# Two expert layers on one core: the first weights in eight chunks on two queues

## The chip, the core and the metric

The kernel runs on one core of one Trainium2 chip. A core has TensorE (PE, matrix products), VectorE (DVE), ScalarE (ACT), GpSimd (POOL) and SyncE (SP), which only issues transfers here. Transfers (DMAs) are issued from SyncE and ScalarE and run on 16 DMA engines that the two share. The metric is the device time of one execution in microseconds (us); less is better.

## The reference

There are 128 samples x of 128 rows and 1024 columns, and for each sample a role among three (the values 1 and 2 occur). Two layers follow each other; each picks its weights by the sample's role:

```python
h = einsum('bsh,bhk->bsk', x, W_down[role]) + b_down[role]   # 1024 -> 512
h = gelu(h)
u = einsum('bsk,bkh->bsh', h, W_up[role]) + b_up[role]       # 512 -> 1024
y = x + u
x = layernorm(y) * gamma[role] + beta[role]
```

All numbers are float32. The second layer has weights of its own and the same form.

## The kernel before, in words

**Tiling.** The samples are sorted by role on the chip and taken in pairs of one role, 63 full pairs and one pair of left-over samples. The run has four phases: down and up of the first layer, down and up of the second. A phase goes over all pairs. The product of a pair is computed by a scheme of seven half-size products in place of eight, from sums of parts of x (`Sd`, written by `winograd_sums`, L418 to L421, mostly on GpSimd) and of parts of the weights (`T1` to `T4`, written for the first phase by `first_sum`, L171, on VectorE). Weights of three "places", one for each role in order of frequency, live in the tile `wall`.

**The first pair is special.** Its role is the most frequent one (`role_0`), and its two samples are the first two with it (`first_two`), both known early. It is computed plainly (`plain`, L576 to L594): for each of the two samples a bias product (L584, one row), then eight products of 128 by 128 with 128 by 512 (L587), each with the next block j of 128 rows of W_down; then the activation on ScalarE (L591). A float32 product is two passes on TensorE, so the profile counts 16 for a sample. The weights for this come in two transfers of 1 MB, `load_rows(0, ...)` on ScalarE's queue and `load_rows(1, ...)` on SyncE's (L148): partition p holds rows 8p to 8p + 7 of W_down, of which each transfer takes four. x comes in four transfers of 128 KB for each sample (`quartered`, L404, in rows of 1 KB), and VectorE turns it (L547, `turn`), for the first pair in halves of four blocks.

**Sorting.** Before that, VectorE works out the order of the samples in some 40 short steps (L274 to L361). Three results come through TensorE by `gathered` (a product, L338, and a copy to a row, L340): `perm` (which sample sits in which slot), `role_of` (which role has which place) and `place` (which place a slot has; read only from the 22nd pair on). Between these, `zeros` (L262) issues products of zeros into banks whose results nobody reads.

**Order.** The order of the work is written out by hand: `at(time, step)` (L835) puts a step on a list, the list is emptied in order of time, and each instruction is bound to follow the one before it on its engine (L987). The units of time are steps, seven to a pair, and say nothing of microseconds. The code that sorts runs before the list. The steps at the head of the first phase:

```python
at(-31, lambda: load_rows(0, 0, nc.scalar))
at(-30.5, load_bias_row)
at(-29, lambda: load_rows(1, 0, nc.sync))
at(-26, lambda: load_bias([0], nc.scalar))
at(0.3, lambda: subtract(slice(0, 1)))
for t, name in zip((-8.7, -2.5, 4.6, 4.7), ("T1", "T2", "T3", "T4")):
```

(L961 to L966.) x of the first pair is issued at steps -30 and -28, of the second and third pair from -19 on. Transfers carry one of eight semaphores, by turns, and a transfer waits before it is issued until the one that last had its semaphore has landed; so about eight are under way at a time.

Of the kernel before, what the change touches and what calls it, by code (L numbers as in the profile page):

```python
# [13 lines left out]
ALU = mybir.AluOpType  # L14
ENG = mybir.EngineType
# [4 lines left out]
P = 128  # L20
SQ = 32
NQ = P // SQ
# [4 lines left out]
def kernel(  # L27
# [29 lines left out]
    nc = tc.nc  # L57
    B, S, H = x.shape
    R, _, K = layers[0][0].shape
# [25 lines left out]
    def flat(tag, bufs, name, size=2048):  # L85
        return work.tile([P, size], F32, tag=tag, name=name, bufs=bufs)
# [51 lines left out]
    rows_of = [  # L138
        wall[:, 2 * k : 2 * k + 2]
        .rearrange("p k n -> p (k n)")  # L140
        .rearrange("p (r j h c) -> p r j h c", r=R, h=2, c=K // 2)
        for k in range(2)
    ]

    def load_rows(k, place, queue):
        role = reg(role_of, place, [queue.engine], R - 1) if place else reg(role_0, 0, [queue.engine], R - 1)
        src = layers[0][0][ds(role, 1)].rearrange("o (p m) c -> p (o m) c", p=P)
        queue.dma_start(rows_of[k][:, place].rearrange("p j h c -> p j (h c)"), src[:, ts(k, NQ)])  # L148

    first_weights = {  # L150
        "B11": Half(rows_of[0], 0),
# [8 lines left out]
    def first_sum(name, place):  # L160
        b11, b12, b21, b22 = (rows_of[k][:, :, :, h] for k in range(2) for h in range(2))
        t1, t2, t4 = (
            first_weights[n].v.rearrange("p r (j c) -> p r j c", c=K // 2) for n in ("T1", "T2", "T4")
        )
        o, a, b = {
            "T1": (t1, b12, b11),
            "T2": (t2, b22, t1),
            "T3": (b12, b22, b12),
            "T4": (t4, b21, t2),
        }[name]  # L170
        nc.vector.tensor_tensor(o[:, place], a[:, place], b[:, place], ALU.subtract)  # L171

    class Sums:
# [85 lines left out]
    def zeros(tags):  # L259
        for t in tags:  # L260
            ps = psum.tile([P, 512], F32, tag=t, name=f"{t}_zero", bufs=3)
            nc.tensor.matmul(ps, zero[:, 0:P], zero[:, 0:512], start=True, stop=True)  # L262
# [3 lines left out]
    def bank_a(name):  # L266
        return psum.tile([P, 512], F32, tag="a", name=name, bufs=2)
# [4 lines left out]
    iota_r, ones_r = iota_row[:, 0:R], ones[:, 0:R]  # L272
# [18 lines left out]
    ps = bank_a("row_ps")  # L291
    nc.tensor.matmul(ps[:, 0 : B + 2 * R], ones[0:1, 0:P], row[0:1], start=True, stop=True)

    zeros("bbbbbbbb")
    role_row, key = ps[:, 0:B], f32(R)
    counts = f32(R + 1)

# [3 lines left out]
    role_0 = const.tile([1, 1], I32, name="role_0")  # L301
# [8 lines left out]
    role_col, rank, own_key = f32(1), f32(1), f32(1)  # L310
# [18 lines left out]
    onehot = f32(B)  # L329
# [4 lines left out]
    def gathered(name, values, where):  # L334

        ps = bank_a(name + "_ps")
        n = where.shape[1]
        nc.tensor.matmul(ps[0:SQ, 0:n], values, where, start=True, stop=True)  # L338
        t = const.tile([1, n], I32, name=name)
        nc.vector.tensor_copy(t, ps[0:1, 0:n])  # L340
        return t

    perm = gathered("perm", wide, onehot)
    zeros("bbb")

    place_r, key_r, at_place = f32(1)[0:R], f32(1)[0:R], f32(R)[0:R]
    nc.vector.tensor_scalar(at_place, iota_r[0:R], iota_col[0:R], None, ALU.is_equal)
# [7 lines left out]
    role_of = gathered("role_of", wide[0:R], at_place)  # L355
    zeros("bbb")

    own_place, wide_place = f32(1), f32(SQ)
    counted(own_place, key, own_key, ALU.is_gt, ones_r)
    nc.vector.tensor_copy(wide_place, own_place.to_broadcast((P, SQ)))  # L360
    place = gathered("place", wide_place, onehot)  # L361
    zeros("bbbb")

    def reg(t, s, engines, top):
        return nc.values_load(
            t[0:1, s : s + 1],
            engines=engines,
            min_val=0,
            max_val=top,
            skip_runtime_bounds_check_because="computed on the chip, always in this range",  # L370
        )

    def set_places(item, engines):

        n = item.n
        if n < NFIRST:
            item.places = [0, 0]
        elif n < NPAIR:
            item.places = [reg(place, 2 * n, engines, R - 1)] * 2
        else:  # L380
            item.places = [reg(place, 2 * n + s, engines, R - 1) for s in range(2)]

    def samples(n, engine):
        return [reg(perm, 2 * n + s, [engine], B - 1) for s in range(2)]
# [11 lines left out]
    first_rows = const.tile([P, 1, K], F32, name="first_rows")  # L396
    bias_row = first_rows[0:1, 0]

    def quartered(t, srcs):

        for s, src in enumerate(srcs):
            n = src.shape[-1] // NQ
            for q in range(NQ):
                nc.sync.dma_start(  # L404
                    t[s][ts(q, SQ)], src[:, ts(q, n)].rearrange("(a t) c -> t a c", t=SQ)
                )

    def x_of(layer, n, engine):
        if layer:
            return [mid[n][s] for s in range(2)]  # L410
        return [x[ds(i, 1)].rearrange("o s h -> (o s) h") for i in samples(n, engine)]
# [26 lines left out]
    def bank(t, tag):  # L438
        return psum.tile([P, 512], F32, tag=t, name=f"{t}{tag}", bufs=BANKS[t])
# [77 lines left out]
    class Down:  # L517
# [7 lines left out]
        def load(self):  # L525
            if self.among_weights:


                block = self.ph.weights[ORDER[self.m]].v
                self.xq = [block[:, 1 + s] for s in range(2)]  # L530
            else:
                self.xq = [flat("q", 4, f"xq{self.tag}_{s}", H) for s in range(2)]
            self.xq = [t.rearrange("p (a c) -> p a c", a=NQ) for t in self.xq]
            if self.early:
                quartered(self.xq[0:1], [self.early_x(0, ENG.SP)])
                return
            self.srcs = x_of(self.layer, self.n, ENG.SP)
            quartered(self.xq[0:1], self.srcs[0:1])

        def load_rest(self):  # L540
            quartered(self.xq[1:2], [self.early_x(1, ENG.SP)] if self.early else self.srcs[1:2])
# [34 lines left out]
        def plain(self):  # L576


            self.ps = [None, None]

            def half(s, k):
                if k == 0:
                    self.ps[s] = bank("a", f"{self.tag}_{s}")
                    nc.tensor.matmul(self.ps[s], ones[0:1, 0:P], bias_row, start=True, stop=False)  # L584
                for j in range(NQ):
                    rows = rows_of[k][:, 0, j].rearrange("p h c -> p (h c)")
                    nc.tensor.matmul(  # L587
                        self.ps[s], self.a[:, s, NQ * k + j], rows, start=False, stop=k == 1 and j == NQ - 1
                    )
                if k == 1:  # L590
                    nc.scalar.activation(self.h[s], self.ps[s], AF.Gelu)  # L591

            steps = [(4 * s + 2 * k, lambda s=s, k=k: half(s, k)) for s in range(2) for k in range(2)]
            return steps + [(0.1 + k / 10, lambda k=k: self.turn(1, ts(k, NQ))) for k in range(2)]  # L594

        def products(self):
            return [(-0.5, self.first)] + (self.plain() if self.early else item_products(self, K // 2))
# [237 lines left out]
    def at(time, step):  # L835
        heapq.heappush(events, (time, next(count_), step))
# [117 lines left out]
    ph = phases[0]  # L954
    ph.bias, load_bias, subtract = bias_table(ph.vectors[0], 2)

    def load_bias_row():
        r = reg(role_0, 0, [ENG.Activation], R - 1)
        nc.scalar.dma_start(bias_row, ph.vectors[0][ds(r, 1), :])

    at(-31, lambda: load_rows(0, 0, nc.scalar))  # L961
    at(-30.5, load_bias_row)
    at(-29, lambda: load_rows(1, 0, nc.sync))
    at(-26, lambda: load_bias([0], nc.scalar))
    at(0.3, lambda: subtract(slice(0, 1)))
    for t, name in zip((-8.7, -2.5, 4.6, 4.7), ("T1", "T2", "T3", "T4")):  # L966
        at(t, lambda name=name: first_sum(name, 0))
    at(14.7, lambda: load_bias(range(1, R)))
    at(20.7, lambda: subtract(slice(1, R)))
# [48 lines left out]
```

## Time and profile before

| What | Value |
|---|---|
| median of 3 runs | 3129.63 us (3129.15 to 3130.18) |
| the profiled execution | 3130.06 us |
| its span in the profile | 3128.3 us |
| TensorE busy | 3112.7 us (99%) |
| VectorE busy | 1975.8 us (63%) |
| GpSimd busy | 1777.3 us (57%) |
| first pass of the first pair's product | at 15.02 us |
| first pass of the second pair's product | at 31.81 us |
| TensorE clock from 16 to 19 us | 0.50 of full |

In lines of the timeline the first number is the start, the second the time to the end of the group, both in us; then the engine (`PEld` is the load of TensorE's stationary operand, `SPq` and `ACTq` are issues of transfers), the line of the kernel, the operation, what it writes and reads, the shape, and in brackets how long the engine was idle before and what it then waited for. Lines of waits give the engine and line that waited, whom for, the total in us, the times and the longest.

### The profile page before, as it was taken

To read this page: it belongs to the slowest core of one execution; us is meant where nothing else is said; L and a number is where in the kernel's file an instruction comes from. 1 tells how busy PE (TensorE), PEld (TensorE's weight loads), DVE (VectorE), ACT (ScalarE), POOL (GpSimd) and SP (SyncE) were. 2 spreads that over 40 slices of the span, in tenths; PEclk is the share of its full clock that TensorE was granted. 3 is DMA by queue.
4 is the path that set the end of the run, shared out by engine and by line. 5 is a ranking of instruction groups with operands and counts; after the bars stand their busy time and mean duration, and the time that the engine had idled before them with its cause. 6 is when DMAs were issued, how large, how long until landed. Compare 5 with 4: busy or idle time off the path is not lost.

```text
span 3128.3 us, 42229 instructions
## 1 busy us (share of the span) xinstructions
PE 3112.7 (99%) x10796; PEld 2047.8 (65%) x10796; DVE 1975.8 (63%) x2807; ACT 1203.5 (38%) x2816; POOL 1777.3 (57%) x1391
## 2 busy tenths in 40 slices
PE   9999999999999999999999999999999999999999
PEld 6888888888544444444478888888884444444443
DVE  6554544544678777777864444444447877777777
ACT  1222222222454555454432222222224545454544
POOL 3545344444577767777654343444436777677775
PEclk9999999999999999999999999999999999999999
DMA  8778788876786565656687555555567765656564
GB/s 218 196 216 209 212 206 210 213 209 196 272 288 240 211 227 208 225 212 226 225 224 179 146 130 131 130 127 138 126 183 275 280 239 206 227 207 226 211 227 176
DMA packets 429735, 642.21 MB, mean 205 GB/s; under 512 B 35778, under 2 KB 305603, under 8 KB 428356
## 3 DMA queue, kind: packets, MB, share of 16 engines
q1 hardware_dynamic: 428930, 637.15, 66.2%
q8 instruction: 102, 1.67, 0.2%
q10 hardware_dynamic: 578, 2.36, 0.2%
q14 instruction: 125, 1.02, 0.1%
HBM read 405.02 MB, written 234.36 MB: 204 GB/s over the span
## 4 chain that ended last, share of the span: by engine, by line
PE 49%; POOL 1%; issue 0%; DMA 0%; SPq 0%; DVE 0%; ACT 0%; DVEq 0%; POOLq 0%; ACTq 0%
PE bu L427 14%; PE bd L427 14%; PE eu L427 7%; PE ed L427 7%; PE au L427 3%; PE ad L427 3%; POOL ou L809 0%; SPq L404 0%; DMA hd<-hd 0%; POOL Sd L420 0%; POOL Sd L418 0%; DMA wall<-mid 0%; POOL varu L794 0%; POOL xTd L419 0%; DVE ou L712 0%
## 5 line engine op out<-in xcount | busy, mean ns | idle before, releaser
L427 PE MATMUL bu<-wall,hTu 128*128 (+1 forms) x2048 | 921.3, 592 | 0.0
L547 DVE STREAM_TRANSPOSE xTd<-xqd 128x1024 f32<-128x1024 f32 (+1 forms) x252 | 504.9, 2071 | 350.7 <-PE bd L427 283.8
L427 PEld LDWEIGHTS bu<-wall,hTu 128*128 128x128 f32 x2048 | 389.1, 190 | 487.2 <-issue 456.6
L418 POOL TENSOR_TENSOR Sd<-xTd 128x512 f32<-128x512 f32 x124 | 159.7, 1288 | 790.4 <-DVE xTd L547 782.7
L794 POOL TENSOR_TENSOR varu<-varu,mhalf 128x1 f32<-128x1 f32 x254 | 329.6, 1298 | 393.8 <-ACT varu L793 393.8
L427 PE MATMUL bd<-wall,xTd 128*128 (+1 forms) x2064 | 487.1, 379 | 1.8 <-ACT bd L445 1.8
L427 PE MATMUL eu<-wall,hTu 128*128 (+1 forms) x1040 | 488.0, 592 | 0.0
L427 PE MATMUL bd<-wall,Sd 128*128 (+1 forms) x2000 | 472.8, 379 | 2.2 <-ACT hd L606 1.6
L427 PEld LDWEIGHTS bd<-wall,xTd 128*128 128x128 f32 x2064 | 392.0, 190 | 57.5 <-ACT bd L445 2.6
L427 PEld LDWEIGHTS bd<-wall,Sd 128*128 128x128 f32 x2000 | 379.7, 190 | 56.5 <-issue 2.6
L801 DVE SCALAR_TENSOR_TENSOR ou<-xu,meanu,tables 128x1024 f32<-128x1024 f32 x253 | 325.3, 1286 | 138.3 <-ACT ou L792 120.0
L611 ACT ACTIVATE hd<-hd 128x256 f32<-128x256 f32 x379 | 157.6, 416 | 534.5 <-DVE hd L610 534.4
L427 PEld LDWEIGHTS eu<-wall,hTu 128*128 128x128 f32 x1040 | 197.6, 190 | 247.4 <-issue 218.8
L788 ACT ACTIVATE partu<-statu 128x2 f32<-128x2 f32 x254 | 51.6, 203 | 728.7 <-DVE xu L690 728.7
L809 POOL TENSOR_TENSOR ou<-ou,tables 128x1024 f32<-128x1024 f32 x126 | 296.9, 2356 | 0.0
L792 ACT ACTIVATE ou<-xu,meanu 128x1024 f32<-128x1024 f32 x254 | 291.7, 1148 | 8.4
L681 DVE TENSOR_TENSOR xu<-bu,xu 128x512 f32<-128x512 f32 x256 | 176.1, 688 | 119.1 <-PE bu L427 119.1
L427 PE MATMUL ed<-wall,xTd 128*128 (+1 forms) x1064 | 251.0, 379 | 0.0
L418 POOL TENSOR_TENSOR hTu<-hTu 128x256 f32<-128x256 f32 x126 | 198.1, 1572 | 70.8 <-DVE hTu L656 49.0
L427 PE MATMUL au<-wall,hTu 128*128 (+1 forms) x504 | 236.8, 592 | 0.0
L427 PE MATMUL ed<-wall,Sd 128*128 (+1 forms) x1000 | 236.3, 379 | 0.1
L427 PE MATMUL ad<-wall,xTd 128*128 (+1 forms) x1000 | 236.2, 379 | 0.0
(135 smaller groups left out, 3383.1 us busy)
## 6 DMA issues: line engine op xcount, KB each, us to landing
xqd<-in_x_dram SPq DMA_DIRECT2D x512, 128.0 KB, 3.3
hd<-hd SPq DMA_DIRECT2D x256, 256.0 KB, 2.4
xu<-in_x_dram SPq DMA_DIRECT2D x128, 512.0 KB, 3.8
mid<-ou SPq DMA_DIRECT2D x128, 512.0 KB, 4.2
xu<-mid SPq DMA_DIRECT2D x128, 512.0 KB, 3.8
out_dram<-ou SPq DMA_DIRECT2D x125, 512.0 KB, 3.8
hqu<-hd SPq DMA_DIRECT2D x244, 256.0 KB, 5.0
xqd<-mid SPq DMA_DIRECT2D x488, 128.0 KB, 3.8
```

What stands on the lines that cost most here:

```text
L418: engine.tensor_tensor(dst[:, 1], a11, a21, ALU.subtract)
L427: nc.tensor.matmul(ps[:, 0:cols], a[:, j], w.rhs(r, j, cols), start=start and j == 0, stop=j == n - 1, skip_group_check=True,)
L547: nc.vector.transpose(self.a[:, s, chunks].rearrange("p j (t a) -> p j a t", t=SQ), self.xq[s].rearrange("p a (i j) -> p j a i", i=SQ)[:, ...
L611: nc.scalar.activation(y, y, AF.Gelu)
L681: nc.vector.tensor_tensor(y, ps, y, ALU.add)
L788: nc.scalar.mul(part, self.stat[:, s], -1.0 / H)
L792: nc.scalar.activation(box["o"], self.x[:, s], AF.Square, bias=m, accum_out=v)
L794: nc.gpsimd.tensor_tensor(v, v, mhalf[:, 0:1], ALU.pow)
L801: nc.vector.scalar_tensor_tensor(box["o"], self.x[:, s], box["m"][:, 0:1], row(self.ph.gamma), ALU.add, ALU.mult)
L809: nc.gpsimd.tensor_tensor(o, o, row(self.ph.beta), ALU.add)
```

## The change

Four things change, all at the head of the first phase.

1. The first place's weights come in eight transfers of 256 KB, one for each block of the first pair's products, in the order in which the products read them: blocks 0, 2, 4, 6 and 7 on ScalarE's queue, 1, 3 and 5 on SyncE's. A row of a transfer is 2 KB.
2. The first sample's x is issued half on SyncE's and half on ScalarE's queue. The role's register is loaded once for each queue.
3. `place` is found later: the count and the copy on VectorE (`own_places`) after the turns of the first sample, the product and its row (`places_in_order`) after the fourth product of the first sample. Its four products of zeros are left out; the group before `perm` has 14 in place of 8, the one after it 4 in place of 3.
4. On VectorE, the turns of the second sample come at step 1.1 in place of 0.1, `T2` follows them (step 2.6 in place of -2.5), and the difference of the bias follows that (2.7 in place of 0.3).

```diff
+    def load_first_rows(j, queue):
+
+        src = rows_in_dram(first_role(queue.engine))
+        queue.dma_start(rows_of[j // NQ][:, 0, j % NQ].rearrange("p h c -> p (h c)"), src[:, j])
...
-    zeros("bbbbbbbb")
+    zeros("bbbbbbbbbbbbbb")
...
     perm = gathered("perm", wide, onehot)
-    zeros("bbb")
+    zeros("bbbb")
...
-    own_place, wide_place = f32(1), f32(SQ)
-    counted(own_place, key, own_key, ALU.is_gt, ones_r)
-    nc.vector.tensor_copy(wide_place, own_place.to_broadcast((P, SQ)))
-    place = gathered("place", wide_place, onehot)
-    zeros("bbbb")
+    own_place, wide_place, place = f32(1), f32(SQ), []
+
+    def own_places():
+        counted(own_place, key, own_key, ALU.is_gt, ones_r)
+        nc.vector.tensor_copy(wide_place, own_place.to_broadcast((P, SQ)))
+
+    def places_in_order():
+        place.append(gathered("place", wide_place, onehot))
...
-    def quartered(t, srcs):
+    def quartered(t, srcs, quadrants=range(NQ), queue=nc.sync):
...
             if self.early:
-                quartered(self.xq[0:1], [self.early_x(0, ENG.SP)])
+
+                for k, queue in enumerate((nc.sync, nc.scalar)):
+                    quartered(self.xq[0:1], [self.early_x(0, queue.engine)], (2 * k, 2 * k + 1), queue)
                 return
...
-            return steps + [(0.1 + k / 10, lambda k=k: self.turn(1, ts(k, NQ))) for k in range(2)]
+            return steps + [(1.1 + k / 10, lambda k=k: self.turn(1, ts(k, NQ))) for k in range(2)]
...
+    @functools.cache
+    def first_role(engine):
+        return reg(role_0, 0, [engine], R - 1)
+
     def load_bias_row():
-        r = reg(role_0, 0, [ENG.Activation], R - 1)
-        nc.scalar.dma_start(bias_row, ph.vectors[0][ds(r, 1), :])
-
-    at(-31, lambda: load_rows(0, 0, nc.scalar))
+        nc.scalar.dma_start(bias_row, ph.vectors[0][ds(first_role(ENG.Activation), 1), :])
+
+
+    at(-31, lambda: load_first_rows(0, nc.scalar))
     at(-30.5, load_bias_row)
-    at(-29, lambda: load_rows(1, 0, nc.sync))
+    for j in range(1, 7):
+        at(-29 + j / 10, lambda j=j: load_first_rows(j, nc.sync if j % 2 else nc.scalar))
+    at(-27, lambda: load_first_rows(7, nc.scalar))
     at(-26, lambda: load_bias([0], nc.scalar))
-    at(0.3, lambda: subtract(slice(0, 1)))
-    for t, name in zip((-8.7, -2.5, 4.6, 4.7), ("T1", "T2", "T3", "T4")):
+    at(-8.75, own_places)
+    at(1, places_in_order)
+    at(2.7, lambda: subtract(slice(0, 1)))
+    for t, name in zip((-8.7, 2.6, 4.6, 4.7), ("T1", "T2", "T3", "T4")):
```

More of the change, by code (lines that the diff above doesn't have):

```diff
@@ L1 @@
+import functools
 import heapq
@@ L145, in load_rows, with rows_in_dram @@
     def load_rows(k, place, queue):
-        role = reg(role_of, place, [queue.engine], R - 1) if place else reg(role_0, 0, [queue.engine], R - 1)
-        src = layers[0][0][ds(role, 1)].rearrange("o (p m) c -> p (o m) c", p=P)
+        src = rows_in_dram(reg(role_of, place, [queue.engine], R - 1))
         queue.dma_start(rows_of[k][:, place].rearrange("p j h c -> p j (h c)"), src[:, ts(k, NQ)])
+    def rows_in_dram(role):
+        return layers[0][0][ds(role, 1)].rearrange("o (p m) c -> p (o m) c", p=P)
+    def load_first_rows(j, queue):
+        src = rows_in_dram(first_role(queue.engine))
+        queue.dma_start(rows_of[j // NQ][:, 0, j % NQ].rearrange("p h c -> p (h c)"), src[:, j])
     first_weights = {
@@ L378, in set_places @@
         elif n < NPAIR:
-            item.places = [reg(place, 2 * n, engines, R - 1)] * 2
+            item.places = [reg(place[0], 2 * n, engines, R - 1)] * 2
         else:
-            item.places = [reg(place, 2 * n + s, engines, R - 1) for s in range(2)]
+            item.places = [reg(place[0], 2 * n + s, engines, R - 1) for s in range(2)]
     def samples(n, engine):
@@ L397 @@
     bias_row = first_rows[0:1, 0]
-    def quartered(t, srcs):
+    def quartered(t, srcs, quadrants=range(NQ), queue=nc.sync):
         for s, src in enumerate(srcs):
             n = src.shape[-1] // NQ
-            for q in range(NQ):
-                nc.sync.dma_start(
+            for q in quadrants:
+                queue.dma_start(
                     t[s][ts(q, SQ)], src[:, ts(q, n)].rearrange("(a t) c -> t a c", t=SQ)
```

## The prediction

> **What bounds the kernel now.** I read the page's busy shares first, then who TensorE waited for over the whole span, then the timeline of the first 40 us, then stages of 1 us for clock and DMA. The shares:
>
> ```profile
> PE 3112.7 (99%) x10796; PEld 2047.8 (65%) x10796; DVE 1975.8 (63%) x2807; ACT 1203.5 (38%) x2816; POOL 1777.3 (57%) x1391
> ```
>
> TensorE fills the span, so the end moves only if its first real product starts sooner, if it runs slower somewhere, or if a wait comes or goes. The waits of TensorE over the whole run:
>
> ```profile
> PE perm_ps L338 <- DVE eps L332: 1.9, 1, 1.9
> PE bd L427 <- ACT bd L445: 1.8, 2, 1.2
> PE b_zero L262 <- POOL zero L257: 1.7, 1, 1.7
> PE bd L427 <- ACT hd L606: 1.6, 2, 1.3
> PE ad L587 <- DVE xTd L547: 1.0, 1, 1.0
> PE bu_end L737 <- POOL ou L799: 0.7, 1, 0.7
> ```
>
> After the first products the remaining waits add up to under 5 us in 3,100: whatever the head gains or loses arrives at the end almost whole. The head, in the timeline:
>
> ```profile
> 5.51 0.40 ACTq L148 DMA_DIRECT2D wall<-in_L_cond_W_down_dram  x1
> 6.29 2.15 SPq L404 DMA_DIRECT2D xqd<-in_x_dram  x4
> 10.71 0.22 PE L338 MATMUL role_of_ps<-sorting 3*32 3x3 f32 x2 [0.45 <-DVE sorting L354]
> 12.92 1.12 PE L584 MATMUL ad<-first_rows,sorting 1*128 1x512 f32 x2
> 13.84 2.13 DVE L547 STREAM_TRANSPOSE xTd<-xqd 128x512 f32<-128x512 f32 x2 [1.50 <-DMA xqd<-in_x_dram]
> 15.02 8.83 PE L587 MATMUL ad<-wall,xTd 128*128 128x512 f32 x16 [0.98 <-DVE xTd L547]
> 24.84 7.13 PE L587 MATMUL ad<-wall,xTd 128*128 128x512 f32 x16
> 31.81 1.89 PE L427 MATMUL bd<-wall,xTd 128*128 128x256 f32 x8
> ```
>
> The last wait to end before the first product is that for x: issued at 6.29 to 8.44, turned from 13.84. And the first sample's 16 passes take 8.76 us (15.02 to the next bias product at 23.78), the second's the same work in 6.97 (24.84 to 31.81). The stages say why (columns: stage, then busy time of PE, PEld, DVE, ACT, POOL, granted clock, DMA share, GB/s):
>
> ```profile
> 14.00:15.00 1.00, 0.04 (x1) 0.00 (x0) 1.00 (x2) 0.00 (x0) 0.00 (x0) 1.00 1.00 418
> 15.00:16.00 1.00, 0.98 (x2) 0.49 (x3) 1.00 (x2) 0.00 (x0) 0.00 (x0) 0.85 1.05 265
> 16.00:17.00 1.00, 1.00 (x2) 0.33 (x1) 1.00 (x1) 0.00 (x0) 0.00 (x0) 0.50 1.01 245
> 17.00:18.00 1.00, 1.00 (x3) 0.37 (x2) 0.97 (x2) 0.00 (x0) 0.00 (x0) 0.50 1.09 253
> 18.00:19.00 1.00, 1.00 (x3) 0.48 (x2) 0.31 (x1) 0.00 (x0) 0.00 (x0) 0.50 1.14 219
> 19.00:20.00 1.00, 1.00 (x4) 0.51 (x3) 0.00 (x0) 0.00 (x0) 0.00 (x0) 0.94 1.01 206
> ```
>
> Lost to the clock: 0.15 + 3 x 0.50 + 0.06 = 1.7 us. The DMA engines are full from 9 us on, so the order of the bytes matters as much as their number.
>
> [...] TensorE stood idle at 7.17 to 9.10 (1.9 us) and at 14.04 to 15.02 (1.0 us). [...] beside the weights' 8 KB rows on the other ring, x's 1 KB rows took 5.5 to 5.7 us to land, while 2.8 is the least in the first 45 us. [...] 206 to 236 GB/s where 1 KB rows run alone (18 to 22 us), up to 418 where 8 KB rows do.
>
> **The change, part by part.** Times are of the profiled execution (3130.06 us, span 3128.3, so 1.8 outside it; 0.4 above the median 3129.63, from which I subtract).
>
> *Start of the first product.* It needs TensorE's own chain and x. TensorE: the 14 zero products run 5.11 + 14 x 0.257 = 8.7, before perm at 9.10; the four after perm end at about 10.5, before role_of at 10.71; three more from 10.86 (0.82) end at 11.7; the place product and its four zeros (11.61 to 12.99) are gone. The bias product takes 1.06 (23.78 to 24.84), so TensorE is ready at 12.74. x: half of it is issued on ScalarE behind the first chunk (5.51 to 5.91), the bias row (about 0.5; its second register load falls away) and a register load: about 7.0 and 7.6, against 8.12 for the last quarter now. In front of it on both rings now lie 256 KB of weights, not 1 MB. Landing takes 2.8 (least) to 5.7 us (as now), so 10.5 to 13.4; I take 3.9, near the median 3.7, so 11.5; a first half-turn of 1.13 and the hand-over give 12.7. VectorE is free for it at 11.15, since own_places (0.27 + 0.18) now stands behind the turns. I take 12.9: 2.1 us gained, between 0.1 and 2.3.
>
> *The clock.* [...] I expect full clock: 1.7 gained, or nothing.
>
> *The place product* now costs TensorE 0.41 between the fourth and fifth chunk (from 11.61 now). Its operand is ready at about 11.5 + 2.1 + 0.5 = 14.1, the slot comes at 16.3: no wait. On VectorE its copy (0.28) waits for it until 16.8; behind it stand the turns of the second x, which land later still (below): hidden. It frees an accumulator bank for the second sample's bias product at 20.3: hidden.
>
> *Chunks.* Two transfers of 1 MB in 8 KB rows become eight of 256 KB in 2 KB rows. From 1 KB at 220 GB/s (74 ns per row and engine) and 8 KB at 400 (328 ns), a straight line gives 110 ns for 2 KB: about 300 GB/s, an estimate. So 2.1 MB take 7.0 us instead of 5.2: 1.8 us more of DMA time; at the 1 KB speed it would be 9.5. Each product (0.86 us per chunk) needs its chunk from 12.9 on, the last at 19.3. x and weights, 2.6 MB, take 7.0 + 2.4 from 6.3, so 15.7, and with x of the second sample between them about 17. Some chunks are issued late, because an issue waits for the DMA eight places back: chunk 2 for chunk 0 (about 9.5), chunk 5 for a quarter of x (11.5). Both are over 2 us ahead of need. Cost nothing; if a chunk is late, 0 to 2.5.
>
> *Second x, T2, bias difference.* These issues stand behind three chunks on SyncE and wait for those places; the last waits for chunk 5 (about 14.5) and lands at 18 to 19. Now it lands at 20.6. Turned in 1.1 + 1.1 it is needed at 21.4. T2 (1.2) and the bias difference (0.39) come after and are needed only at the second pair's third product. Hidden, with 1 to 2 us to spare. On ScalarE the bias table waits behind six more issues, about 12.5 instead of 11.8, and its first reader comes near 24.
>
> *The second and third pair.* Gain can be lost here: VectorE's row of work (turns 22.96 to 27.38, sums, T3, T4 to 32.9, turns of the third pair) hangs on x of the second pair, which lands at 25.3 because the DMA engines are full. Now the third pair's first product (38.71) finds its first half turned at 34.88: 3.8 to spare. Its third product (45.62) finds GpSimd's sum at 40.94: 4.7. Since 4.4 MB at the mixed rate end at about 24, I expect that row of work no later than now: cost nothing up to a gain of 3.8.
>
> *Sum.* 12.9 + 6.97 + 0.41 + 1.06 + 6.97 = 28.3 for the second pair's first product, now 31.81: 3.5 us less. **3129.63 - 3.5 = 3126.1.** With TensorE's bound of 12.74 the most is 3.7.
>
> **Rivals.** (1) *The clock halves again*[...]. 3126.1 + 1.7 = 3127.8. (2) *x or a chunk comes late*: [...] x on ScalarE's ring lands as slowly as now (13.4), so products start at 14.6, or chunks in 2 KB rows come one by one. 1 to 2.5 us lost: 3127.1 to 3128.6. (3) *Slower*: small rows and issues waiting for places delay x of the second pair, and VectorE's row of work with it. It decides from the point where that work is 3.8 us later than now, so x landing after 29.1. At the 1 KB speed for all weights it would land near 26.5 and cost under 1 us of the gain; to be slower, the DMA engines would also have to stand idle for 2.6 us. At 31 us, about 3131.5. (4) That the change does not take place can be ruled out: the program's list of instructions shows the eight chunks, the two queues and the moved place product.
>
> **How the numbers follow.** Likeliest 0.60, its own range 3125.5 to 3127.0; clock 0.17; late x or chunk 0.14; slower 0.07; something else 0.02. Leaving out the slower case and the upper end of the late one gives 3125.3 to 3128.9. A measurement of this kernel tells about 0.2% from no change, here 6.3 us. No case reaches that: the gain is capped near 3.7, the slower case near 2. So faster 0.02, within 0.95, slower 0.03, the outer two for what I have not seen.
>
> **What would show it.** In the timeline after: the bias product near 11.7; turns of x from about 11.5; the first product with a chunk near 12.9, without a gap above 0.5 before it; clock 1.00 from 12 to 20; the place product near 16.3; the second pair's first product near 28.3; in TensorE's waits no new line of a chunk or of the third pair's turns. The prediction is wrong if x is turned after 13, if a stage shows 0.50, if TensorE waits for chunks 2 to 7, or if the second x is turned after 21.

## The result and the profile after

The changed kernel takes 3133.12 us (median of 22 runs, 3131.07 to 3135.71), the kernel before 3129.29 (22 runs, 3128.08 to 3131.95). The ratio is 1.0013, with a 95% interval of 1.0007 to 1.0019: 3.8 us slower, where 3.5 us faster was forecast. The profiled execution took 3131.07 us, the quickest of the changed kernel; its span is 3129.3 us.

The head of the profile after, in the timeline (start, time, engine, line, what is written and read):

```profile
12.73 2.13 DVE L560 STREAM_TRANSPOSE xTd<-xqd 128x512 f32<-128x512 f32 x2 [1.29 <-DMA xqd<-in_x_dram]
13.91 5.40 PE L600 MATMUL ad<-wall,xTd 128*128 128x512 f32 x8 [0.85 <-DVE xTd L560]
19.24 0.41 PE L346 MATMUL place_ps<-sorting 128*32 128x128 f32 x2
19.68 0.28 DVE L348 CAST place<-place_ps 1x128 int32<-1x128 f32 x1 [3.37 <-PE place_ps L346]
21.37 2.13 DVE L560 STREAM_TRANSPOSE xTd<-xqd 128x512 f32<-128x512 f32 x2 [1.41 <-DMA xqd<-in_x_dram]
23.41 1.18 DVE L179 TENSOR_TENSOR wall<-wall 128x1024 f32<-128x1024 f32 x1
31.23 1.89 PE L438 MATMUL bd<-wall,xTd 128*128 128x256 f32 x8
```

The first product starts 1.1 us sooner (13.91 against 15.02), the second pair's first product 0.6 us sooner (31.23 against 31.81). Half of the gain of the start is taken by the place product on TensorE's way: the first sample's products, up to the next bias product, now take 9.30 us (13.91 to 23.21) and took 8.76, both with a half clock that costs 1.7 us. The first sample's x is turned from 12.7, the second's from 21.4, later than before (20.64), and T2 (1.18) follows it. The 0.6 us are lost a little later. The same view, at the third pair's first product (L438, `bd`, at 39.35):

```profile
38.19 0.38 DVE L623 TENSOR_TENSOR hd<-ad,hd 128x256 f32<-128x256 f32 x1
38.61 0.42 ACT L624 ACTIVATE hd<-hd 128x256 f32<-128x256 f32 x1 [4.74 <-DVE hd L623]
38.93 0.36 ACT L456 COPY bd<-tables 128x256 f32<-128x256 f32 x1
39.35 1.99 PE L438 MATMUL bd<-wall,xTd 128*128 128x256 f32 x8 [1.05 <-ACT bd L456]
```

and the same four steps of the kernel before, whose first three the prediction left out:

```profile
36.74 0.38 DVE L610 TENSOR_TENSOR hd<-ad,hd 128x256 f32<-128x256 f32 x1
37.16 0.42 ACT L611 ACTIVATE hd<-hd 128x256 f32<-128x256 f32 x1 [2.72 <-DVE hd L610]
37.48 0.37 ACT L445 COPY bd<-tables 128x256 f32<-128x256 f32 x1
38.71 1.89 PE L427 MATMUL bd<-wall,xTd 128*128 128x256 f32 x8
```

The third pair's first product adds to a bank that ScalarE has filled with the bias (the seed, L445 before, L456 after). On ScalarE the seed stands behind the second pair's activation; this waits for an addition on VectorE; and the addition stands behind the turns of the third pair, at the end of VectorE's row of work that starts with the turns of the second sample. Before, the seed was there at 37.85, 0.86 us ahead of the product. After, VectorE is 1.45 us later, and TensorE waits 1.05 us. Of the 1.45 us, 0.73 are the later x of the second sample (21.37 against 20.64); the rest is T2's new place (1.18), less some 0.5 us that VectorE no longer stands idle at the second pair's turns (22.96 to 27.38 before; 4.00 us in one go after). The wait of 1.05 us is the new one among TensorE's waits:

```profile
PE bd L438 <- ACT bd L456: 3.1, 3, 1.2
PE bd L438 <- ACT hd L619: 1.8, 2, 1.5
PE ad L600 <- DVE xTd L560: 0.9, 1, 0.9
PE bu_end L750 <- POOL ou L812: 0.7, 1, 0.7
```

(three waits for a seed, of which two lie at the change from the first layer to the second, as before; of 3.1 us, 1.05 are new.) No chunk is waited for at the first products. The clock was half again there (columns as in the prediction, the third number from the end is the clock):

```profile
14.00:15.00 1.00, 1.00 (x2) 0.55 (x3) 0.97 (x4) 0.00 (x0) 0.00 (x0) 0.69 1.11 265
15.00:16.00 1.00, 1.00 (x2) 0.34 (x1) 1.00 (x2) 0.00 (x0) 0.00 (x0) 0.50 1.13 230
16.00:17.00 1.00, 1.00 (x2) 0.34 (x1) 0.31 (x1) 0.00 (x0) 0.00 (x0) 0.50 1.05 217
17.00:18.00 1.00, 1.00 (x3) 0.48 (x2) 0.00 (x0) 0.00 (x0) 0.00 (x0) 0.60 1.02 279
```

But this profile explains no more than some 1 us, and the medians differ by 3.8. So a second profile of each kernel was needed.

### The profile page after: what moved, and what is told of

Same layout as the page of the kernel before. It is cut to its first block, busy times and chain, and to the rows that moved or that the text cites. A ratio compares the mean times of both kernels' runs of the same rounds, so it can differ in the third digit from the quotient of the medians.

```text
span 3129.3 us, 42254 instructions
## 1 busy us (share of the span) xinstructions
PE 3114.6 (100%) x10799; PEld 2048.2 (65%) x10799; DVE 1975.5 (63%) x2807; ACT 1203.5 (38%) x2816; POOL 1775.7 (57%) x1391
## 4 chain that ended last, share of the span: by engine, by line
PE 49%; POOL 1%; issue 0%; SPq 0%; DMA 0%; DVE 0%; ACT 0%; DVEq 0%; POOLq 0%; ACTq 0%
PE bu L438 14%; PE bd L438 14%; PE eu L438 7%; PE ed L438 7%; PE au L438 3%; PE ad L438 3%; POOL ou L822 0%; SPq L415 0%; POOL Sd L431 0%; DMA hd<-hd 0%; POOL Sd L429 0%; DMA wall<-mid 0%; POOL varu L807 0%; POOL xTd L430 0%; SPq L828 0%
## 5 line engine op out<-in xcount | busy, mean ns | idle before, releaser
L438 PE MATMUL bu<-wall,hTu 128*128 (+1 forms) x2048 | 921.3, 592 | 0.0
L438 PEld LDWEIGHTS bu<-wall,hTu 128*128 128x128 f32 x2048 | 389.1, 190 | 487.2 <-issue 456.6
L438 PE MATMUL bd<-wall,xTd 128*128 (+1 forms) x2064 | 487.2, 379 | 3.1 <-ACT bd L456 3.1
L438 PE MATMUL eu<-wall,hTu 128*128 (+1 forms) x1040 | 488.0, 592 | 0.0
L438 PE MATMUL bd<-wall,Sd 128*128 (+1 forms) x2000 | 472.8, 379 | 2.1 <-ACT hd L619 1.8
L438 PEld LDWEIGHTS bd<-wall,xTd 128*128 128x128 f32 x2064 | 391.9, 190 | 59.2 <-ACT bd L456 4.3
L438 PEld LDWEIGHTS bd<-wall,Sd 128*128 128x128 f32 x2000 | 379.7, 190 | 56.4 <-issue 2.8
L438 PEld LDWEIGHTS eu<-wall,hTu 128*128 128x128 f32 x1040 | 197.6, 190 | 247.5 <-issue 218.8
L438 PE MATMUL ed<-wall,xTd 128*128 (+1 forms) x1064 | 251.0, 379 | 0.0
L438 PE MATMUL au<-wall,hTu 128*128 (+1 forms) x504 | 236.8, 592 | 0.0
L438 PE MATMUL ed<-wall,Sd 128*128 (+1 forms) x1000 | 236.3, 379 | 0.1
L438 PE MATMUL ad<-wall,xTd 128*128 (+1 forms) x1000 | 236.2, 379 | 0.0
```

The costliest lines, as they stand in the source:

```text
L438: nc.tensor.matmul(ps[:, 0:cols], a[:, j], w.rhs(r, j, cols), start=start and j == 0, stop=j == n - 1, skip_group_check=True,)
```

## The experiments

Two theories. **A:** VectorE's row of work, from the second sample's turns on, has become late; the third pair waits for the seed at its end, and what is gained or lost on TensorE before is of no account. **B:** the loss lies at the first products, in the clock and the chunks. A rival within A, **C:** the row is late through the place product, whose copy VectorE waits for, and not through the transfers.

### Both kernels once more

The changed kernel, no edit:

> The changed kernel once more, for a second profile. Theory A (the third pair's first product waits for its seed on ScalarE, which waits for an addition on VectorE that stands behind the turns of the third pair): a wait of TensorE for ScalarE before that product, at least 1.0 us as in the first profile, and about 2 us longer where the execution is near the median of 3133.1. Theory B (the loss lies at the first products: clock and chunks): the time from the first product to the second pair's first product grows by 2 us and the later wait stays at 1.0.

Measured: 3133.68 us, ratio to before 1.0014 (1.0007 to 1.0021). The profiled execution took 3134.36 us, near the median. In the timeline:

```profile
14.22 5.40 PE L600 MATMUL ad<-wall,xTd 128*128 128x512 f32 x8 [1.47 <-DVE xTd L560]
22.99 2.12 DVE L560 STREAM_TRANSPOSE xTd<-xqd 128x512 f32<-128x512 f32 x2 [2.72 <-DMA xqd<-in_x_dram]
31.54 1.89 PE L438 MATMUL bd<-wall,xTd 128*128 128x256 f32 x8
40.54 0.36 ACT L456 COPY bd<-tables 128x256 f32<-128x256 f32 x1
40.95 2.81 PE L438 MATMUL bd<-wall,xTd 128*128 128x256 f32 x8 [2.35 <-ACT bd L456]
43.55 2.81 PE L438 MATMUL bd<-wall,Sd 128*128 128x256 f32 x8
46.20 1.89 PE L438 MATMUL ad<-wall,xTd 128*128 128x256 f32 x8
```

The second x is turned at 23.0, and the third pair waits 2.35 us. What comes behind the wait costs nearly as much again: the third pair's first two products take 2.60 and 2.65 us, and a product without a wait takes 1.73. The stages of this execution (the third number from the end is the clock):

```profile
41.00:42.00 1.00, 1.00 (x5) 0.90 (x6) 1.00 (x1) 0.47 (x2) 0.92 (x2) 0.99 0.90 234
42.00:43.00 1.00, 1.00 (x4) 0.82 (x3) 1.00 (x2) 0.00 (x0) 0.92 (x2) 0.50 1.13 219
43.00:44.00 1.00, 1.00 (x4) 0.73 (x4) 1.00 (x1) 0.00 (x0) 0.98 (x1) 0.50 1.13 216
44.00:45.00 1.00, 1.00 (x4) 0.82 (x3) 0.16 (x1) 0.00 (x0) 0.94 (x1) 0.50 1.15 331
```

The clock is half behind the wait, and 1.7 us more are lost here.

The kernel before, no edit:

> The kernel before once more, for a second profile: its first one (3130.1) lies above its own median of 3128.9. Theory A: at its median the first products run without the half clock or x lands sooner, so the second pair's first product comes about 1 us before 31.8, the third pair's first product still without a wait of more than 0.5. If it is as in the first profile up to the third pair, the median differs for a reason outside the head, and part of the measured loss would too.

Measured: 3128.54 us, ratio 0.9999 (0.9990 to 1.0007). The profiled execution took 3128.87 us.

```profile
14.86 7.13 PE L587 MATMUL ad<-wall,xTd 128*128 128x512 f32 x16 [0.81 <-DVE xTd L547]
19.84 2.14 DVE L547 STREAM_TRANSPOSE xTd<-xqd 128x512 f32<-128x512 f32 x2 [1.70 <-DMA xqd<-in_x_dram]
29.94 1.89 PE L427 MATMUL bd<-wall,xTd 128*128 128x256 f32 x8
36.84 0.36 ACT L445 COPY bd<-tables 128x256 f32<-128x256 f32 x1
37.26 1.99 PE L427 MATMUL bd<-wall,xTd 128*128 128x256 f32 x8 [0.25 <-ACT bd L445]
```

Here the kernel before has the full clock at its first products (1.00 in each stage from 14 to 20 us; 16 passes in 7.13 us, 8.83 in the first profile), and the second pair starts at 29.9, not 31.8. The third pair already waits 0.25 us for its seed: the row on VectorE and TensorE's work were level, and nothing was to spare. (The expectation had the second pair about 1 us sooner; it was 1.9, and the third pair took back 0.4.)

Between these two executions the books close. Second pair's first product: 31.54 against 29.94, +1.60, of which the half clock is 1.7, the place product 0.5 (what is left of the first sample's products, 9.30 us against 7.06), the earlier start of the first product (14.22 against 14.86) -0.64. Wait for the seed: 2.35 against 0.25, +2.10. Half clock behind the wait: +1.7. Together 5.4; the last product of the run that waits (`bu_end`, the last but one) starts at 3122.80 against 3117.41, 5.39 later. The seed itself comes 3.7 us later (L456 at 40.54 against L445 at 36.84), of which 3.15 are the later x of the second sample (22.99 against 19.84); whatever TensorE had gained at the head would only have made the wait longer.

The start of the third pair's first product carries most of the time in all runs. That start, the start of the `bu_end` named above, and their difference, from each run's timeline:

| Run | third pair | `bu_end` | difference |
|---|---|---|---|
| before / once more | 38.71 / 37.26 | 3118.62 / 3117.41 | 3079.91 / 3080.15 |
| after / once more | 39.35 / 40.95 | 3119.50 / 3122.80 | 3080.15 / 3081.85 |
| T2 put back | 40.24 | 3120.42 | 3080.18 |
| addition put first | 39.21 | 3120.09 | 3080.88 |
| zeros behind the bias | 41.01 | 3123.45 | 3082.44 |
| chunks alone | 39.95 | 3121.13 | 3081.18 |
| places alone | 39.56 | 3119.76 | 3080.20 |
| both repairs | 38.34 | 3120.00 | 3081.66 |
| rows of 4 KB | 41.66 | 3121.86 | 3080.20 |
| second x early | 45.08 | 3125.24 | 3080.16 |
| x first, 64 partitions | 42.99 | 3124.02 | 3081.03 |
| x first, halves on ScalarE | 38.64 | 3119.22 | 3080.58 |
| the same, kept busy | 37.61 | 3118.11 | 3080.50 |

In six of the fifteen profiles the difference is 3080.15 to 3080.20. In "once more" of the changed kernel it is larger by the half clock behind the wait, in "zeros" it is larger by 2.3 us, of which the waits for ScalarE's `hd` (2.4 us in all) make 0.6 and the rest is not explained, in the others it is off by up to 1.5 us, in the largest of them through later waits of TensorE: those for `hd` add up to 2.8 us in "chunks alone" and 3.0 in "both repairs", against 1.6 to 1.8 in the profiles of the two kernels. The two runs with the addition put first on the changed kernel have 0.53 of it behind the fourth product of the second pair.

### T2 put back

```diff
-    for t, name in zip((-8.7, 2.6, 4.6, 4.7), ("T1", "T2", "T3", "T4")):
+    for t, name in zip((-8.7, -2.5, 4.6, 4.7), ("T1", "T2", "T3", "T4")):
```

> Only the difference T2 goes back in front of the second sample's turns. A: VectorE idles there anyway (3.4 and 1.4 us in the profile after), so its row of work gets 1.2 us shorter and the time falls by 1.0 to 1.2 us against the changed kernel, to about 3132. B: no change, since T2 is not needed by the first products: 3133.

Measured: 3132.35 us, ratio 1.0011 (1.0004 to 1.0017), 1.3 us under the changed kernel measured beside it (3133.68); the intervals overlap. In the profile T2 fills time in which VectorE waited, and the addition starts at 39.09, not 39.80. The wait for the seed is 1.64, not 2.35, and no half clock follows it (the third pair's first two products take 1.83 and 1.72 us). So T2's new place is a part of the loss, by the medians of the size that A gives. In the profiles the row from the second x's turn to the addition is only 0.56 us shorter (22.84 to 39.09, against 22.99 to 39.80), since VectorE now waits for the second pair's x.

### The addition put first

```diff
-            prepare = {1: 4.5 - base, 2: 8.6 - base}.get(m, kind.PREPARE) if k == 0 else kind.PREPARE
+            prepare = {1: 4.5 - base, 2: 9.3 - base}.get(m, kind.PREPARE) if k == 0 else kind.PREPARE
```

> Only the addition of the second pair's second product goes in front of the third pair's turns on VectorE. A: the seed no longer stands behind 4 us of turns; the third pair's first product then waits at most for its own first half of turns, 2.2 us earlier. The time falls by 1 to 3 us against the changed kernel, to 3130 to 3132. B: no change, 3133.

Measured: 3131.99 us, ratio 1.0010 (1.0003 to 1.0016), 1.7 us under the changed kernel; the intervals overlap here too. Nothing but VectorE's order of one addition and two turns is altered, and the wait before the third pair is gone, although the second x is turned at 23.4 here:

```profile
36.34 0.41 DVE L623 TENSOR_TENSOR hd<-ad,hd 128x256 f32<-128x256 f32 x1
37.49 1.89 PE L438 MATMUL ed<-wall,xTd 128*128 128x256 f32 x8
39.21 1.89 PE L438 MATMUL bd<-wall,xTd 128*128 128x256 f32 x8
```

That is what theory B could not give. It does not bring the kernel back to 3129: TensorE's own way (first product at 14.99, half clock with its first eight passes in 5.40 us, place product) now sets the third pair, and 0.53 us are waited for at 46.81. So the row is one part of the loss, and not the whole.

### Zeros behind the bias

Four zero products after the first bias product:

```diff
                     nc.tensor.matmul(self.ps[s], ones[0:1, 0:P], bias_row, start=True, stop=False)
+                    if s == 0:
+                        zeros("bbbb")
```

> Four more products of zeros between the first bias product and the first products[...]. A: if the clock stays full, the second pair's first product comes up to 1.7 us sooner, but the wait before the third pair grows by as much: 3133, unchanged. B: the 1.7 us arrive at the end: 3131.4. If the clock halves all the same, it says nothing between the two, and the gap is not its cause.

Measured: 3133.69 us, ratio 1.0014 (1.0008 to 1.0021): unchanged. The first products ran at full clock (13.99 to 17.6 for the first four blocks, against 14.22 to 19.55 once more), as A and B both asked, and the 1.7 us of B did not arrive at the end. But not in the way that A expected: TensorE then waited 0.54 us for the last chunk and 0.71 for the second x, ran part of the second sample at half clock (16 passes in 8.59 us, 7.13 at full), and so had lost the gain before the second pair (32.65, against 31.54 once more). It waited 1.29 for the seed all the same. This execution, 3135.63, is the slowest of the run's 21. The run shows that the first products alone do not bring the time back while the second x is late; it does not decide between A and B at the third pair.

### The chunks alone, the places alone

The change with places, zero products and VectorE's order as before:

```diff
-    zeros("bbbbbbbbbbbbbb")
+    zeros("bbbbbbbb")
...
-    at(-8.75, own_places)
-    at(1, places_in_order)
-    at(2.7, lambda: subtract(slice(0, 1)))
+    at(0.3, lambda: subtract(slice(0, 1)))
...
```

> The first weights in eight chunks and the first x on two queues, as in the change; the places, the zero products and VectorE's order as in the kernel before. Theory A (the second sample's x is late because its issues wait for chunks to land, and VectorE's row of work with it): second x turned at 21.4 or later, a wait of TensorE before the third pair's first product, and a time near that of the run with T2 put back, 3132 (3131 to 3133). Rival C (the place product, with VectorE's copy waiting for it, makes the second x late): second x turned at 20.6 or earlier, 3129 or less.

Measured: 3131.23 us, ratio 1.0009 (1.0001 to 1.0018). In the profiled execution, which at 3132.95 lies above the median:

```profile
22.68 2.13 DVE L557 STREAM_TRANSPOSE xTd<-xqd 128x512 f32<-128x512 f32 x2 [1.17 <-DMA xqd<-in_x_dram]
39.95 1.99 PE L435 MATMUL bd<-wall,xTd 128*128 128x256 f32 x8 [2.04 <-ACT bd L453]
```

The second x is turned at 22.68, and the third pair waits 2.04 us for its seed. The first products ran at full clock (16 passes in 7.13 us), the second pair started at 30.84, and it was of no use. Theory A's case: the transfers alone make the row late.

The other half, with weights and x as in the kernel before:

```diff
-    at(-31, lambda: load_first_rows(0, nc.scalar))
+    at(-31, lambda: load_half(0, nc.scalar))
...
+    at(-29, lambda: load_half(1, nc.sync))
...
```

> The other half alone: places, zero products and VectorE's order as in the change; the weights in two transfers and x on one queue, as before. A: second x turned near 20.6 as before; T2 behind it makes VectorE's row of work 1.2 us longer against a slack of 0.86 before the third pair, so 0.3 to 0.6 us are lost, unless the full clock at the first products moves them ahead: 3129 (3128 to 3130). C: all of the loss, 3133.

Measured: 3131.71 us, ratio 1.0008 (0.9999 to 1.0016), more than A expected and less than C. In the timeline (VectorE and TensorE):

```profile
15.36 5.38 PE L598 MATMUL ad<-wall,xTd 128*128 128x512 f32 x8 [2.62 <-DVE xTd L558]
20.66 0.41 PE L346 MATMUL place_ps<-sorting 128*32 128x128 f32 x2
21.11 0.28 DVE L348 CAST place<-place_ps 1x128 int32<-1x128 f32 x1 [3.39 <-PE place_ps L346]
21.31 2.12 DVE L558 STREAM_TRANSPOSE xTd<-xqd 128x512 f32<-128x512 f32 x2
39.56 1.89 PE L438 MATMUL bd<-wall,xTd 128*128 128x256 f32 x8
```

The second x does not wait for its transfer here but for the copy of the places in front of it, which waits for the fourth product. So what C names does happen: after a late first product and at half clock (eight passes in 5.38 us) the place's copy holds VectorE past the landing of x. But TensorE does not pay for it in this profile: the third pair starts at 39.56 without a wait. The loss here lies on TensorE's own way, which is late by its first product (15.36, behind a wait of 2.62 us for x), the half clock and the place product, which lay in a gap before (second pair at 32.65). In the two profiles of the changed kernel VectorE stood idle behind the copy for 1.41 and 2.72 us until x had landed, so there the transfers set the row, and not C. By the medians the halves cost 2.3 and 2.8 us, both together 3.8 and 4.9 in the two measurements of the change; the interval of the second half includes no change.

### Rows of 4 KB

Four transfers of two blocks each:

```diff
-    at(-31, lambda: load_first_rows(0, nc.scalar))
+    at(-31, lambda: load_pair(0, nc.scalar))
...
-    for j in range(1, 7):
-        at(-29 + j / 10, lambda j=j: load_first_rows(j, nc.sync if j % 2 else nc.scalar))
-    at(-27, lambda: load_first_rows(7, nc.scalar))
+    at(-28.9, lambda: load_pair(1, nc.sync))
+    at(-28.8, lambda: load_pair(2, nc.scalar))
+    at(-28.7, lambda: load_pair(3, nc.sync))
```

> The change with four transfers of 512 KB in rows of 4 KB in place of eight of 256 KB in rows of 2 KB (0 and 2 on ScalarE's queue, 1 and 3 on SyncE's). Four places fewer are taken, so the second x no longer waits for chunks to land. A: its issues are over by 14 us and it is turned by 20.6; the time falls by 2 to 4 us against the change, to 3129 to 3131. If rows of 2 KB and waiting issues are not the cause, it stays at 3133.

Measured: 3133.22 us, ratio 1.0013 (1.0006 to 1.0020). A miss. The first x was now turned from 15.2 (12.7 and 13.0 in the two profiles of the change), so the first product started at 16.41, and the place's copy held the second x until 23.4. The third pair started at 41.66 without a wait for its seed: as with the places alone, TensorE's own way set it, and the run is no test of the waiting issues. Whether x landed later through the larger rows beside it is not shown; there were also twice as many bytes in front of its half on ScalarE's queue.

### The second x in front of chunks 3 and 5

```diff
-                rest = -28 if m == 0 else first + 0.05
+                rest = -28.75 if m == 0 else first + 0.05
```

> The change with the second sample's x issued after chunk 1 and ahead of chunks 3 and 5 on SyncE's queue; nothing else. A: the second x is turned at 20 (behind the place's copy at 19.7) in place of 21.4 to 23, the wait before the third pair shrinks to 1 us or less and draws no half clock behind it: 3130 to 3131.5. Chunks 3 and 5 may come late instead; then TensorE waits for a chunk at the first products, and the time stays at 3133 though the second x is early.

Measured: 3136.82 us, ratio 1.0023 (1.0015 to 1.0031): the second outcome, and worse. Chunk 3 now stands on SyncE behind the second x, whose last issue goes out at 14.54 only; chunk 3 goes out at 15.05, and TensorE and T1 wait for it:

```profile
15.05 0.35 SPq L156 DMA_DIRECT2D wall<-in_L_cond_W_down_dram  x1
22.15 2.08 PE L600 MATMUL ad<-wall,xTd 128*128 128x512 f32 x2 [3.16 <-DMA wall<-in_L_cond_W_down_dram]
22.18 1.22 DVE L179 TENSOR_TENSOR wall<-wall 128x1024 f32<-128x1024 f32 x1 [6.49 <-DMA wall<-in_L_cond_W_down_dram]
```

So the places tie the chunks and x together both ways, and in either of these two orders one of the two is late. The second x was not turned sooner (25.03), since T1 and the place's copy stand ahead of it on VectorE; how early it had landed is not seen.

### Other orders of the transfers

Four runs tried for a version that beats both kernels; none does. *x first, weights by 64 partitions:* x of the first sample ahead of everything, then each half of the weights in 8 KB rows as two transfers of 64 partitions, one on each queue; with T2 and the addition as above.

```diff
-    at(-31, lambda: load_first_rows(0, nc.scalar))
...
+    for k in range(2):
+        for side, queue in enumerate((nc.scalar, nc.sync)):
+            at(-29 + k / 2, lambda k=k, side=side, queue=queue: load_side(k, side, queue))
+    at(-28.8, load_bias_row)
```

> The change with x of the first sample in front of all weights on both queues, the weights in two halves of 8 KB rows, each half as two transfers of 64 partitions, one on each queue; T2 back in front of the second sample's turns, and the addition in front of the third pair's turns. A: x turned from about 10.5, first product near 12.9, second x turned near 18.5, no wait before the third pair; 2 to 4 us less than the kernel before, 3125 to 3127. If x or the second half of the weights comes no sooner this way, 3128 to 3130.

Measured: 3135.57 us, ratio 1.0021 (1.0013 to 1.0030). x was turned at 11.16 (10.5 was expected); but the bias row, 2 KB issued at 8.54 behind the weights, let TensorE wait until 16.79, and T2 waited for the second half until 21.48.

*Both repairs* (T2 put back and the addition first):

```diff
-            prepare = {1: 4.5 - base, 2: 8.6 - base}.get(m, kind.PREPARE) if k == 0 else kind.PREPARE
+            prepare = {1: 4.5 - base, 2: 9.3 - base}.get(m, kind.PREPARE) if k == 0 else kind.PREPARE
...
-    for t, name in zip((-8.7, 2.6, 4.6, 4.7), ("T1", "T2", "T3", "T4")):
+    for t, name in zip((-8.7, -2.5, 4.6, 4.7), ("T1", "T2", "T3", "T4")):
```

> Both repairs together on the changed kernel: T2 in front of the second sample's turns and the addition in front of the third pair's turns. A: no wait for the seed; what is left of the loss is the first products' start and clock and the place product (0.4): 3130 to 3132, and less than or as much as either repair alone (3132.0 and 3132.4).

Measured: 3131.36 us, ratio 1.0008 (1.0000 to 1.0017). No wait before the third pair, which starts at 38.34. Against the second profile of the kernel before that is 1.1 us late, and the later waits named under the table add 1.5. So the changed kernel is late on two ways that meet at the third pair, VectorE's row and TensorE's own; repairing the row brings back about half of the loss.

*x first, then the weights in halves on ScalarE's queue alone*, the bias row ahead of them, with both repairs:

```diff
-    at(-31, lambda: load_first_rows(0, nc.scalar))
...
+    at(-29.5, load_bias_row)
+    at(-29, lambda: load_half(0))
+    at(-28.9, lambda: load_half(1))
```

> The change with all transfers in another order: x of the first sample in front on both queues, then on SyncE's queue only x of the second sample, on ScalarE's the bias row and the weights in their two transfers of 1 MB in 8 KB rows, first half first; with both repairs of the run before. A: x turned by 11.5, the first half landed by 13, the second by 16.5, second x turned by 18.5; first product near 13.2, second pair's first product near 29, no wait before the third pair: 3125.5 to 3127.5. If the first half lands no sooner than x does now (13.8): 3128 to 3129.

Measured: 3130.77 us, ratio 1.0005 (0.9997 to 1.0013). x is turned at 11.48 and the second x at 20.82, VectorE's addition waits 2.76 us for TensorE and not the other way, but the first half of the weights lands at 14.4 only (13 was expected), and the clock halves (eight passes in 5.30 us).

*The same with TensorE kept busy*, the place product back in front and two zero products behind the bias:

```diff
-    at(-8.75, own_places)
-    at(1, places_in_order)
...
+                    if s == 0:
+                        zeros("bb")
```

> The transfers of the run before (x first, then the weights in halves on ScalarE's queue), but the place product back among the zero products as in the kernel before, and two more zero products after the first bias product, so that TensorE is never idle before the first product. If the gap causes the half clock: full clock at the first products, the second pair's first product near 29.6, the third pair's near 36.5 without a wait, and a time of 3128 to 3128.6, at or just under the kernel before. If the clock halves all the same: 3130.

Measured: 3130.17 us, ratio 1.0005 (0.9997 to 1.0013). Full clock in the profile (1.00 from 10 to 25 us), and the third pair at 37.61 without a wait, though the first half of the weights landed 1.1 us later than in the run before. TensorE was not kept busy all the same: it stood idle for 1.02 us until these weights landed. By their intervals neither of the last two can be told from the kernel before; both medians lie above it.

## Why the prediction was wrong

**Start of the first product:** the direction was right, the size was not. Forecast 12.9; it was 13.9 and 14.2, because x was turned from 12.7 and 13.0 and not from 11.5: its last quarter was issued at 7.85, not 7.6, and landed 4.7 us later in the first profile in place of 3.9.

**The clock:** wrong in two ways. That it would be full was the author's estimate, and no trace of the kernel before showed what makes it halve. A gap above 0.5 us was there all the same (0.85 and 1.47 us), and rival 1's half clock came in both profiles of the change (the first eight passes in 5.40 us). That the gap brings it is not shown: with both repairs TensorE had a gap of 1.50 us there and full clock (3.70). And the 1.7 us were taken for a loss of every execution of the kernel before, from one profile: its second profile has none, at a gap of 0.81 us there and 0.98 in the first.

**The place product:** it cost TensorE 0.5 us and not 0.41, and its slot (16.3) came at 19.2. That VectorE's waiting copy is hidden held in the changed kernel (the second x lands later still); in the run with the places alone the copy did hold the second x.

**Chunks:** that no chunk is waited for at the first products was right in both profiles, which had a late start and half clock. At full clock (the first eight passes in 3.70 us, or 16 in 7.13) TensorE did wait 0.54 us for the last chunk in one profile (zeros behind the bias) and not in two others (chunks alone, both repairs); so there was little margin, and that it held was in part luck. From 14 to 18 us 217 to 279 GB/s came in, where 300 were estimated for rows of 2 KB.

**Second x, T2, bias difference:** here it failed first. The second x was to land at 18 to 19; it was turned from 21.4 and 23.0. Its last issue was put at 14.5 and went out at 15.16 in the first profile (13.00 before), since three of its four issues (12.4, 13.98 and 15.16) wait for chunks, which land at 12.4, 14.0 and 15.2:

```profile
13.00 0.32 SPq L404 DMA_DIRECT2D xqd<-in_x_dram  x1
15.16 0.32 SPq L415 DMA_DIRECT2D xqd<-in_x_dram  x1
```

(before and after.) It then took 6.1 us to land, where the forecast's 18 to 19 allowed 3.5 to 4.5. In the kernel before the parts of the second x that the trace tells had taken 6.3 to 7.5 us, so this term was too small by the profile at hand. T2 was called hidden, because TensorE needs it late; but it stands in VectorE's row, in front of everything that the third pair needs, and cost 1.2 us of that row.

**The second and third pair:** here it failed decisively. The slack was read as 3.8 us, from the turns and the sums, the two inputs of the product that come from x. The third input, the bank seeded by ScalarE, was not followed back: its engine's order leads to an activation, to an addition on VectorE, and behind the turns. That slack was 0.86 us in the profile at hand, and nothing in the second one. So the row costs time from 0.86 us on, or at once, and not from 3.8 us on. Rival 3 named the row, but put its delay on the x of the second pair (VectorE did not wait for that in either profile of the change; the second sample's x and T2 came first), and had a wrong point from which it decides and so a chance of 0.07.

**What no step had:** a wait may be paid twice. In the execution near the median a half clock of 1.7 us followed the wait of 2.35 us.

**Signs and range:** of the four signs named for a wrong prediction three came: x turned after 13 (in the second profile), a stage at 0.50, the second x turned after 21. That the whole stays within 0.2% came true, but every term of the sum is small against those 6.3 us, so it says nothing for the mechanism. The lower end of the range, 3125.3, comes out of none of the cases; the lowest has 3125.5.

## What to carry to other kernels

Slack before a product is the least over all its inputs, each followed back through the order of its engine: also the bank it adds to, and whatever stands in front of the instruction that fills it. A transfer that is cut in eight takes eight places in a line of transfers that wait for each other, so look at what is issued behind it, and on which engine's row that hangs. And where a gain is about as large as a loss that one profile has and the next has not (here 1.7 us of half clock), one profile is not the kernel: take a second one of each before counting it.

## What the runs showed of the hardware

The clock answered waits of nearly the same length differently. In front of the first products it halved behind gaps of 0.85 and 1.47 us (the two profiles of the change) and 0.98 (the kernel before), and stayed full behind 0.81 (the kernel before once more), 0.91 (chunks alone) and 1.50 us (both repairs): the first eight passes took 5.40 us in the two profiles of the change and 3.70 with both repairs, the first 16 took 8.83 in the kernel before, 7.13 in its second profile and with the chunks alone. Before the third pair it halved behind 2.35 us (once more, changed kernel) and stayed full behind 1.05, 1.64 and 2.04 us (the change, T2 put back, chunks alone): the first product there took 2.81 us after the first of these waits and 1.99 after the other three, to the end of the group. So the length of the gap alone does not decide; what does is open.

The same transfers in the same order landed 1.6 us apart in two executions of one kernel, by the turns that wait for them (second x turned at 21.37 and 22.99).

A transfer of 2 KB issued behind a 512 KB transfer of 8 KB rows on the same queue kept its reader waiting until 8 us after its issue (8.54 to 16.79). Weights in transfers of 64 partitions on both queues (512 KB each) landed no faster for that: T2 found the second half at 21.48, against 18.46 (x first, halves on ScalarE) where each half was one transfer of 1 MB on one queue.
